# The first Walsh-Hadamard transform of a quantized feed-forward layer: one butterfly level on VectorE instead of inside the matrix products

## The chip, the cores and the metric

The kernel runs on one core of a Trainium2 chip. The metric is the device time of one execution in microseconds (us); lower is better. A profile of one execution comes beside the times. Its engines are called PE (the matrix unit, TensorE), PEld (PE's weight loads), DVE (VectorE), ACT (ScalarE), POOL (GpSimd) and SP (which here only issues transfers).

## What is computed

The input x has 128 sequences of 32 rows with 256 features, 4096 rows in all. Two layers are added to it one after the other:

```python
# layer 0: a projection with a low-rank adapter per sequence, then a mixture of
# eight experts (the best two per row) with a shared expert
x = x + L0_ffn(L0_cond(x, W, A, Bm, scalings, itok_B_0_6), gate, w1, w2, w3, ws1, ws2, ws3)

# layer 1: a mix of the 32 rows of a sequence, chosen per sequence,
# then a two-layer net on quantized values
h = einsum('bct,bcd->bdt', x, weights[itok_B_1_198])
xq = act_quant(fwht(h))                  # 256 features
h  = square(relu(xq @ weight_quant(w_up).T))
xq = act_quant(fwht(h))                  # 512 features
x  = x + xq @ weight_quant(w_down).T
```

`fwht` is the normalized fast Walsh-Hadamard transform along the features. `act_quant` divides each row by its largest absolute value, scaled to 127, and rounds. `weight_quant` rounds weights to -1, 0 and 1 times a scale.

For 256 features split into halves a and b of 128, and H the 128 by 128 Hadamard matrix, the transform is [aH + bH, aH - bH] / 16. It can also be had as [(a + b)H, (a - b)H] / 16.

## The kernel before

The kernel has three stages in one program.

- Up to about 120 us: projection, routing, and the scatter of each row to the regions of its two experts in device memory.
- Up to about 280 us: the experts' products over 72 tiles of 128 rows, in pairs, with the shared expert for all rows before and after.
- From about 280 us on: layer 1, over 16 groups of 256 rows (`G3` groups, of two tiles of 128 rows each). The change is in this stage.

In the third stage a group g goes through these functions, named here with their main tiles and lines:

- `combine` loads the two expert rows of each row (y2) and adds them to x on POOL (L634).
- `condition` forms, on PE, the mix of the sequences' rows. It comes out transposed, features on the partitions: py (called `pa` in the code, L642), two halves of 128 features, each 256 rows wide. ACT copies both halves to yT (L650).
- `quantize1` makes the transform of 256 features on PE, pf (L658): for each tile of 128 rows two products of 256 columns, one with the first half of the features and [H, H], one with the second half and [H, -H], summed in the accumulation memory. DVE then takes the row maximum m (L668, L670), the scale and its reciprocal ms (L672, L675), and ACT rounds to q1 (L679).
- `worth` squares the scales on POOL (L687, L688).
- `turn1` transposes q1 on PE (pq, L696) and ACT brings it into qT (L700).
- `up` makes the 512 hidden features, pu (L712), in two halves of bank "m". ACT takes the relu (rl, L720), DVE the square (r and pu, L721), and then the sum and the difference of the two halves, c (L722, L723), which is the outer level of the second transform.
- `outer` makes the next level on POOL: b (L730, L731).
- `quantize2` makes the remaining transform with H on PE, pr (L742), products of 128 columns. DVE forms the scale (L749, L753), ACT rounds to q2 (L756).
- `dequant` prepares the last factor on POOL (L763).
- `turn2` transposes q2 (pq, L770; ACT L772).
- `down2` makes the last product pd (L780). DVE scales it and adds x, o (L784), and the result is stored (L787).

A loop over 23 steps calls them in a software pipeline: in step s, `down2` works on group s - 7, `turn2` on s - 6, `quantize2` on s - 5, `outer` on s - 4, `up` on s - 3, `turn1` on s - 2, `quantize1` on s - 1 and `condition` on s. POOL's order is the written order (`manual_schedule`). For PE, DVE, ACT and SP the build orders the instructions by its own estimate of when they can start. On the chip each engine takes its instructions in the order built.

The accumulation memory has two buffers for each tag. Tag "t" serves py, pf and pd alike; "x" serves both pq, "m" pu, "o" pr. A tile that takes a buffer waits until the last reader of the previous one is done.

The Hadamard matrices lie in `cst`, a tile of constants: `had` is H, and `had256` gives [H, H] / 16 and [H, -H] / 16 out of three blocks of 128 columns. The constants come in two transfers (L202, L207), the second amid the loads of the rows of stage 1.

Of the kernel before, what the change touches and what calls it, by code (L numbers as in the profile page):

```python
# [7 lines left out]
F32 = mybir.dt.float32  # L8
# [4 lines left out]
ALU = mybir.AluOpType  # L13
AX = mybir.AxisListType

P = 128
D = 256
# [12 lines left out]
NSLOT = 72  # L30
# [5 lines left out]
SHARED1 = 6  # L36


C_ID, C_H, C_HS, C_TRI, C_E16, C_N16 = 0, 128, 256, 640, 704, 712
C_U, C_EREG, C_EW, C_I, C_T2 = 714, 842, 850, 858, 858 + NSLOT  # L40
NCONST = C_T2 + NT


# [1 line left out]
def tile_kernel(  # L45
# [20 lines left out]
    nc = tc.nc  # L66
# [9 lines left out]
    def bank(tag, name, shape=(P, 512), dtype=F32):  # L76
        return psum.tile(list(shape), dtype, tag=tag, name=name)
# [11 lines left out]
    cst = cpool.tile([P, NCONST], F32, name="cst")  # L89
    ident = cst[:, C_ID : C_ID + P]  # L90
    had = cst[:, C_H : C_H + P]
    had256 = [cst[:, C_HS : C_HS + D], cst[:, C_HS + P : C_HS + P + D]]
    tri = cst[:, C_TRI : C_TRI + 64].rearrange("p (e j) -> p e j", j=E)


# [16 lines left out]
    with tc.tile_pool(name="moe", bufs=1) as moe, tc.tile_pool(name="work1", bufs=2) as work1:  # L112
# [61 lines left out]
        with tc.tile_pool(name="stage", bufs=1) as stage:  # L174
# [50 lines left out]
            for k in range(3):  # L225
                for c in range(2):
# [6 lines left out]
                        start=(c == 0),  # L233
                        stop=(c == 1),
# [386 lines left out]
    work = ctx.enter_context(tc.tile_pool(name="work3", bufs=2, reuse_waits="tile"))  # L621
    TG = 2 * P
    yv = yt.rearrange("(g n p r) d -> g p n r d", n=2, p=P, r=2)

    def x_of(n):
        return xg[n // GT][:, n % GT]
# [9 lines left out]
    def condition(g):  # L636

        pa = bank("t", f"py{g}", (P, 2, TG))
        for i in range(2):
            n = 2 * g + i  # L640
            for k in range(2):
                nc.tensor.matmul(  # L642
                    pa[:, k, i * P : (i + 1) * P],
                    x_of(n)[:, k * P : (k + 1) * P],
                    bd[:, n],
                    start=True,
                    stop=True,
                )
        yT = work.tile([P, 2, TG], F32, tag="yT", name=f"yT{g}")
        nc.scalar.copy(yT, pa)  # L650
        return yT

    def quantize1(g, yT):

        pf = bank("t", f"pf{g}", (P, 2, D))
        for i in range(2):
            for k in range(2):
                nc.tensor.matmul(  # L658
                    pf[:, i],
                    yT[:, k, i * P : (i + 1) * P],  # L660
                    had256[k],
                    start=(k == 0),
                    stop=(k == 1),
                )

        ms = small.tile([P, 2, 2], F32, tag="ms", name=f"ms{g}")
        m = small.tile([P, 2], F32, tag="m", name=f"m{g}")
        nc.vector.tensor_reduce(m, pf, AX.X, ALU.max, apply_absolute_value=True)  # L668

        nc.vector.scalar_tensor_tensor(m, pf[:, :, 0], EPS, m, ALU.max, ALU.max)  # L670
        for i in range(2):
            nc.vector.tensor_scalar(  # L672
                ms[:, 0, i : i + 1], pf[:, i, 0:1], m[:, i : i + 1], 1.0 / QB, ALU.max, ALU.mult
            )
        nc.vector.reciprocal(ms[:, 1], ms[:, 0])  # L675

        q1 = work.tile([P, 2, D], F16, tag="q1", name=f"q1_{g}")
        for i in range(2):
            nc.scalar.activation(  # L679
                q1[:, i], pf[:, i], AF.Identity, bias=half, scale=ms[:, 1, i : i + 1]  # L680
            )
        return q1, ms
# [107 lines left out]
    with tc.manual_schedule(engines={mybir.EngineType.Pool}):  # L790
        for g in range(2):
            combine(g)
        y, q1, qT1, c4, b4, q2, qT2 = {}, {}, {}, {}, {}, {}, {}
        mss, s2s, m2s, dqs = {}, {}, {}, {}
        for s in range(G3 + 7):
            if 0 <= s - 2 < G3:
                s2s[s - 2] = worth(s - 2, mss.pop(s - 2))
            if 0 <= s - 6 < G3:
                dqs[s - 6] = dequant(s - 6, m2s.pop(s - 6), s2s.pop(s - 6))
            if 0 <= s - 7 < G3:  # L800
                down2(s - 7, qT2.pop(s - 7), dqs.pop(s - 7))
            if 0 <= s - 6 < G3:
                qT2[s - 6] = turn2(s - 6, q2.pop(s - 6))
            if 0 <= s - 5 < G3:
                q2[s - 5], m2s[s - 5] = quantize2(s - 5, b4.pop(s - 5), s2s[s - 5])
            if 0 <= s - 4 < G3:
                b4[s - 4] = outer(s - 4, c4.pop(s - 4))
            if s + 2 < G3:
                combine(s + 2)
            if 0 <= s - 3 < G3:  # L810
                c4[s - 3] = up(s - 3, qT1.pop(s - 3))
            if 0 <= s - 2 < G3:
                qT1[s - 2] = turn1(s - 2, q1.pop(s - 2))
            if 0 <= s - 1 < G3:
                q1[s - 1], mss[s - 1] = quantize1(s - 1, y.pop(s - 1))
            if s < G3:
                y[s] = condition(s)


def _constants():  # L820

    import numpy as np

    h = np.ones((1, 1), np.float32)
    while h.shape[0] < P:
        h = np.block([[h, h], [h, -h]])
    c = np.zeros((P, NCONST), np.float32)
    p = np.arange(P)
    e = np.arange(E)
    c[:, C_ID : C_ID + P] = np.eye(P)  # L830
    c[:, C_H : C_H + P] = h

    c[:, C_HS : C_HS + 3 * P] = np.concatenate([h, h, -h], axis=1) / 16.0
    c[:, C_TRI : C_TRI + E * E] = (e[None, :] < e[:, None]).reshape(1, -1)
    c[:, C_E16 : C_E16 + E] = p[:, None] // 16 == e[None, :]
    c[:, C_N16] = p // 16
    c[:, C_U : C_U + P] = p[:, None] < p[None, :]
    c[:, C_EREG : C_EREG + E] = e[None, :] * REG
    c[:, C_EW : C_EW + E] = e[None, :] * WCOL
    c[:, C_I : C_I + NSLOT] = np.arange(NSLOT)[None, :]  # L840

    c[:, C_T2 : C_T2 + NT] = 2 * (np.arange(NT)[None, :] * P + p[:, None]) - NY
    return c


def _layouts(inputs):
# [29 lines left out]
        "cond": v["L1_cond_weights"],  # L876
        "updown": np.stack([up, down], axis=1),
        "consts": _constants(),
    }

# [19 lines left out]
```

## Time and profile before

| what | value |
|---|---|
| median of 3 runs | 405.39 us (404.98 to 406.67) |
| profiled execution | 408.42 us, of which span 406.6 us |
| PE busy | 357.1 us (88%) |
| PEld busy | 281.4 us (69%) |
| POOL busy | 248.5 us (61%) |
| DVE busy | 227.4 us (56%) |
| ACT busy | 163.6 us (40%) |
| chain that ended last | PE 66%, POOL 15%, issue 7%, DVE 5% |
| PE's part of that chain at L658 (pf) | 6% |

The span is the time from the first to the last record of the profiled execution. Busy time is the time in which an engine executed something; an engine can be busy and still not set the time, and one that is idle may only be waiting for another. The chain that ended last is followed backwards from the last instruction, at each step to what released it. In rows of groups, "L658 PE MATMUL pf<-cst,yT" means line 658, engine, operation, output, inputs; "x128" is the number of instructions. Durations of matrix products are modelled and overlap one another, so the distance from one start to the next is the better measure.

### The profile page before, as it was taken

What the parts mean: (1) busy time and instruction counts of PE and PEld (TensorE: products, weight loads), DVE (VectorE), ACT (ScalarE), POOL (GpSimd) and SP (SyncE); (2) the same over time, 40 slices, a digit from 0 to 9 for tenths busy, and PEclk for the clock granted to TensorE, in tenths of its full rate; (3) what the DMA queues carried; (4) which work ended last, traced back from release to release, by engine and by line L of the source; (5) the groups of instructions that cost most, each with busy time, mean ns of one, the idle gap of its engine ahead of it and who ended that gap; (6) DMA issues with size and microseconds to landing.
All of it is one profiled execution on the core that took longest, in us unless ns stands there. A gap on an engine that the chain in (4) does not pass through costs nothing.

```text
span 406.6 us, 6564 instructions
## 1 busy us (share of the span) xinstructions
PE 357.1 (88%) x2055; PEld 281.4 (69%) x2055; DVE 227.4 (56%) x714; ACT 163.6 (40%) x328; POOL 248.5 (61%) x274
## 2 busy tenths in 40 slices
PE   4999999999800499999999989998999999999983
PEld 3677677565500288888787868856788998999772
DVE  1177887996500355555555545434566767757672
ACT  1122222311100034444434433421678777786863
POOL 4028888888887015555556455557898778772650
PEclk9999999999955599999999999999999999999998
DMA  6996359642222735455455431217523242010112
GB/s 230 418 409 220 133 166 248 248 141 83 94 80 96 204 107 164 147 157 164 137 151 153 147 127 71 79 35 250 179 84 119 88 140 94 33 48 28 52 53 77
DMA packets 39025, 57.49 MB, mean 141 GB/s; under 512 B 9293, under 2 KB 28879, under 8 KB 38608
## 3 DMA queue, kind: packets, MB, share of 16 engines
q1 hardware_dynamic: 31744, 39.17, 30.2%
q0 software_dynamic: 6672, 17.84, 12.2%
q8 instruction: 17, 0.28, 0.3%
q14 instruction: 16, 0.13, 0.1%
q10 hardware_dynamic: 576, 0.08, 0.1%
HBM read 33.93 MB, written 24.18 MB: 143 GB/s over the span
## 4 chain that ended last, share of the span: by engine, by line
PE 66%; POOL 15%; issue 7%; DVE 5%; DMA 3%; ACT 2%; SPq 1%; DVEq 0%; POOLq 0%; ACTq 0%
PE pg L556 16%; POOL xs L345 10%; PE pr L742 7%; PE po L582 7%; PE pf L658 6%; PE ph L265 5%; POOL pause L357 4%; PE pt_s L530 3%; PE py L642 3%; PE pd L780 3%; PE pu L712 3%; PE ph L268 3%; PE pa L253 3%; PE phd L573 2%; PE pgs L142 2%
## 5 line engine op out<-in xcount | busy, mean ns | idle before, releaser
L589 POOL DMA_INDIRECT yt<-y,to x72 | 70.1, 973 | 70.0 <-DVE cm L539 21.1
L345 POOL DMA_INDIRECT xs<-hc,dest x64 | 63.5, 992 | 40.2 <-DVE s L278 22.9
L556 PE MATMUL pg<-wall,xTs 128*128 x288 | 77.9, 395 | 3.5 <-DVE xTs L84 2.1
L556 PEld LDWEIGHTS pg<-wall,xTs 128*128 128x128 f32 x288 | 50.3, 193 | 15.4 <-issue 4.6
L564 ACT ACTIVATE sil<-pg,c 128x128 f32<-128x128 f32 x72 | 26.4, 367 | 62.5 <-PE pg L556 52.5
L565 DVE SCALAR_TENSOR_TENSOR hid<-pg,c,sil 128x128 f32<-128x128 f32 x72 | 25.0, 347 | 44.4 <-ACT sil L564 30.5
L530 PE MATMUL pt_s<-cst,xin 128*128 128x128 f32 x144 | 26.1, 286 | 25.5 <-DMA xin<-xs 25.5
L634 POOL TENSOR_TENSOR x<-x,y 128x512 f32<-128x512 f32 x32 | 40.5, 1271 | 6.2 <-PE pgs L142 4.9
L530 PEld LDWEIGHTS pt_s<-cst,xin 128*128 128x128 f32 x144 | 19.1, 147 | 30.7 <-DMA xin<-xs 26.7
L582 PE MATMUL po<-wall,hidT 128*128 x144 | 37.8, 382 | 0.0
L658 PE MATMUL pf<-cst,yT 128*128 128x256 f32 x128 | 34.9, 394 | 1.6 <-ACT yT L650 1.6
L742 PE MATMUL pr<-cst,b 128*128 128x128 f32 x256 | 34.8, 280 | 1.2 <-POOL b L731 0.7
L265 PE MATMUL ph<-WT,xT 128*128 128x264 f32 x128 | 34.9, 397 | 0.0
L269 ACT COPY hc<-ph 128x264 f32<-128x264 f32 x32 | 12.1, 378 | 50.5 <-PE ph L268 35.1
L742 PEld LDWEIGHTS pr<-cst,b 128*128 128x128 f32 x256 | 31.0, 192 | 1.7 <-POOL b L731 0.9
L265 PEld LDWEIGHTS ph<-WT,xT 128*128 128x128 f32 x128 | 25.2, 197 | 8.3 <-issue 3.7
L142 PE MATMUL pgs<-hT,ws 128*128 128x512 f32 x64 | 29.1, 598 | 0.4 <-DVE hT L84 0.4
L582 PEld LDWEIGHTS po<-wall,hidT 128*128 128x128 f32 x144 | 24.4, 190 | 2.2 <-ACT hidT L86 0.3
L658 PEld LDWEIGHTS pf<-cst,yT 128*128 128x128 f32 x128 | 21.5, 191 | 4.3 <-ACT yT L650 2.3
L756 ACT ACTIVATE q<-pr,half,sc 128x512 f16<-128x512 f32 x32 | 23.1, 779 | 2.1 <-DVE sc L753 2.1
L86 ACT COPY xTs<-pt_s 128x512 f32<-128x512 f32 x17 | 9.9, 584 | 34.6 <-PE pt_s L530 32.9
L730 POOL TENSOR_TENSOR b<-c 128x512 f32<-128x512 f32 x16 | 20.3, 1267 | 4.2 <-DVE m L749 2.7
(138 smaller groups left out, 672.9 us busy)
## 6 DMA issues: line engine op xcount, KB each, us to landing
xin<-xs SPq DMA_DIRECT2D x72, 136.0 KB
y<-yt SPq DMA_DIRECT2D x16, 512.0 KB
xT<-in_xT SPq DMA_DIRECT2D x8, 512.0 KB
x<-in_x SPq DMA_DIRECT2D x8, 512.0 KB
out<-o SPq DMA_DIRECT2D x16, 256.0 KB
wall<-in_experts SPq DMA_DIRECT2D x2, 1536.0 KB
yt<-y,to POOLq DMA_INDIRECT x72
xs<-zeros SPq DMA_DIRECT2D x8, 136.0 KB
```

The source lines that it names most:

```text
L142: nc.tensor.matmul(pg, ws13[:, k, i], hT[:, k], start=(k == 0), stop=(k == 1))
L265: nc.tensor.matmul(ph, xT[g][:, k, cols], WT[:, k], start=(k == 0), stop=False)
L345: ins = nc.gpsimd.indirect_dma_start(out=xs, out_offset=bass.IndirectOffsetOnAxis(ap=dest[:, i, n : n + 1], axis=0), in_=hc[g][:, n], in_o ...
L530: nc.tensor.transpose(pt[:, i, k], xin[:, i, k * P : (k + 1) * P], ident)
L556: nc.tensor.matmul(pg[:, i].rearrange("p a f -> p (a f)"), xT[:, i, k], wall[:, bass.ds(w + k * D, D)], start=(k == 0), stop=(k == 1),)
L564: nc.scalar.activation(sil[:, i], pg[:, i, 0], AF.Silu, scale=ci)
L565: nc.vector.scalar_tensor_tensor(hid[:, i], pg[:, i, 1], ci, sil[:, i], ALU.mult, ALU.mult)
L582: nc.tensor.matmul(po[:, i], hT[:, i], wall[:, bass.ds(w + 2 * D, D)], start=True, stop=True)
L589: ins = nc.gpsimd.indirect_dma_start(out=yt, out_offset=bass.IndirectOffsetOnAxis(ap=to[:, i : i + 1], axis=0), in_=y[:, i], in_offset=Non ...
L634: nc.gpsimd.tensor_tensor(v, v, y2[:, :, r], ALU.add)
L658: nc.tensor.matmul(pf[:, i], yT[:, k, i * P : (i + 1) * P], had256[k], start=(k == 0), stop=(k == 1),)
L742: nc.tensor.matmul(pr[:, f * P : (f + 1) * P], b[:, f, i * P : (i + 1) * P], had, start=True, stop=True,)
```

## The change

`condition` no longer copies both halves of py. ACT copies only the second half, to a new tile y1. DVE then writes the sum of the first half (read from the accumulation memory) and y1 to the first half of yT, and their difference to the second half. A DVE operation of this kind reads at most one of its inputs from the accumulation memory here, as the other sums and differences of the kernel do.

`quantize1` multiplies each half of yT by the same matrix H / 16. Each product has 128 columns and writes a part of pf of its own, so nothing is summed in the accumulation memory. There are as many products as before, four for a group. The constants lose two blocks of 128 columns, and the offsets behind them move. Lines from L649 on move by four.

```diff
-C_ID, C_H, C_HS, C_TRI, C_E16, C_N16 = 0, 128, 256, 640, 704, 712
-C_U, C_EREG, C_EW, C_I, C_T2 = 714, 842, 850, 858, 858 + NSLOT
+C_ID, C_H, C_HS, C_TRI, C_E16, C_N16 = 0, 128, 256, 384, 448, 456
+C_U, C_EREG, C_EW, C_I, C_T2 = 458, 586, 594, 602, 602 + NSLOT
...
-    had256 = [cst[:, C_HS : C_HS + D], cst[:, C_HS + P : C_HS + P + D]]
+    hads = cst[:, C_HS : C_HS + P]
...
+        y1 = work.tile([P, TG], F32, tag="y1", name=f"y1_{g}")
         yT = work.tile([P, 2, TG], F32, tag="yT", name=f"yT{g}")
-        nc.scalar.copy(yT, pa)
+        nc.scalar.copy(y1, pa[:, 1])
+        nc.vector.tensor_tensor(yT[:, 0], pa[:, 0], y1, ALU.add)
+        nc.vector.tensor_tensor(yT[:, 1], pa[:, 0], y1, ALU.subtract)
         return yT
...
                 nc.tensor.matmul(
-                    pf[:, i],
+                    pf[:, i, k * P : (k + 1) * P],
                     yT[:, k, i * P : (i + 1) * P],
-                    had256[k],
-                    start=(k == 0),
-                    stop=(k == 1),
+                    hads,
+                    start=True,
+                    stop=True,
                 )
...
-    c[:, C_HS : C_HS + 3 * P] = np.concatenate([h, h, -h], axis=1) / 16.0
+    c[:, C_HS : C_HS + P] = h / 16.0
```

## The prediction

> **What bounds the kernel now.** I read the busy tenths of the page first: PE stands at 9 in nearly all slices, from 285 us on too, where the edited functions run. Then the busy time in stretches of 7 us, about one group of 256 rows.
>
> ```profile
> 323.00:330.00 7.00, 7.00 (x62) 6.30 (x61) 4.41 (x14) 5.17 (x10) 5.27 (x8) 1.00 0.33 112
> ...
> sum 77.00, PE 76.94 PEld 69.70 DVE 52.56 ACT 58.06 POOL 55.50; mean PE 7.00 PEld 6.34 DVE 4.78 ACT 5.28 POOL 5.05
> ```
>
> PE is busy 76.94 of 77 us (302 to 379) at full clock; VectorE has 2.2 us per 7 free, ScalarE 1.7. A busy PE may still hide slack, so next the chain that ended last, for one group (start, length, what):
>
> ```profile
> 319.55 0.87 PE pu L712 x8
> 320.43 0.06 PE pq L696
> 320.48 0.49 PE pf L658 x2
> 320.97 0.17 PE pq L696 x3
> 321.14 1.35 PE pf L658 x6
> 322.49 0.89 PE py L642 x8
> 323.38 0.45 PE pq L770 x8
> 323.83 0.28 PE pr L742 x2
> 324.10 0.98 PE pd L780 x8
> 325.09 1.56 PE pr L742 x14
> 326.65 0.87 PE pu L712 x8
> ```
>
> The chain stays on PE all the way round, 7.10 us from pu to pu. The pieces give true paces, since each ends where the next starts: an fp32 instruction of 128 columns takes 0.89/8 = 0.111 us (py), one of 256 columns 1.84/8 = 0.23 (pf; 0.22 where nothing comes between). Each fp32 product is two such instructions: 128 of L658 for 64 products. The group rows (busy, mean ns | idle before) give single durations, and what the 256-column VectorE and ScalarE work resembles:
>
> ```profile
> L658 PE MATMUL pf<-cst,yT 128*128 128x256 f32 x128 | 34.9, 394 | 1.6 <-ACT yT L650 1.6
> L784 DVE SCALAR_TENSOR_TENSOR o<-pd,dq,x 128x256 f32<-128x256 f32 x32 | 14.8, 473 | 5.1 <-issue 2.9 <-POOL b L730 1.1 <-PE pd L780 1.0
> L722 DVE TENSOR_TENSOR c<-pu,r 128x512 f32<-128x512 f32 x16 | 10.9, 683 | 0.1
> L650 ACT COPY yT<-py 128x512 f32<-128x512 f32 x16 | 9.4, 590 | 11.6 <-PE py L642 11.4
> ```
>
> Last the waits, 302 to 379 us:
>
> ```profile
> POOL s L687 <- DVE ms L675: 19.9, 11, 4.1
> DVE r L721 <- ACT rl L720: 17.2, 10, 2.6
> ACT q L679 <- DVE ms L675: 11.4, 8, 1.6
> ```
>
> The others wait for one another while PE never stops: POOL 1.8 us per group for ms, ScalarE about 1.0, VectorE 1.6. That slack must carry what the change adds.
>
> **What the Trainium skill says.** (1) "TensorE: Matmul & The Clock Gate", Back-to-back issue gap: when warm, N/2.4 + 2.5 ns between products of N columns, so 109 ns at 256. The trace agrees for bf16 (pu: 0.87/8 = 109 ns); an fp32 instruction takes twice that. The same section says that a stream with a weight load per product keeps only 81 ns at 128 columns; the trace has 0.45/8 = 56 ns (pq), so weight loads do not hold this stream. (2) "VectorE: DVE Perf Modes", The TRN2 errata: an fp32 tensor_tensor takes (N + 151)/0.96 ns, 691 at 512 columns (trace: 683) and 424 at 256. (3) "Perfetto Trace Analysis", Tensor Engine Instruction: ScalarE, VectorE and GpSimd are strict FIFOs. The trace fits: ms waits behind both c operations. The last point decides this case.
>
> **The change part by part.** Line numbers are those of before.
>
> *Removed from PE:* half the columns of 128 instructions. Per group pf falls from 1.84 to 8 × 0.111 = 0.89, 0.9 us with the interleaving. If all were paid out: 16 × 0.9 = 14.4 us.
>
> *ScalarE:* the copy has 256 columns for 512. Nearest row: L269, 264 columns from PSUM, 378 ns. So 0.37 for 0.59, 0.22 less per group.
>
> *Added to VectorE:* 32 operations of 256 columns. The trace has no such tensor_tensor; bounds are L565 (128 columns, 347 ns) and L784 (256 columns, 473 ns). L722 less 256 columns at 0.96 GHz is 683 - 267 = 416 ns, near the page's 424. I take 0.42; the next one starts 0.08 earlier (the c pair starts every 0.60), so 0.34 of queue each. VectorE rises from 52.56/11 = 4.8 to 5.5 us per group.
>
> *The wait:* yT needed py and one copy, 0.1 + 0.59. Now y1, a hand-over of about 0.05, then sum and difference: 0.1 + 0.37 + 0.05 + 0.76 = 1.3 at best, plus what stands ahead in VectorE's queue. Waiting for it: pf, and by the bank "t" also pd, since py, pf and pd share two buffers. Before, pd runs inside pr, 0.05 us after the yT copy is done; the build now places it after pu or its first product. Queued behind the pair: ms (L675), for which ScalarE's q1 and POOL's worth and outer wait, and the maxima L749.
>
> *Hidden or nothing:* the constants' DMA carries 256 columns (128 KB) less; at the 418 GB/s of the page's third slice that is 0.3 us, beside PE work, so 0, at most 0.3 gained. There the build also exchanges one xa with a reciprocal and a comparison, and two L265/L268 products: 0, bounds -0.5 to 0.5. SP issues the same DMAs. POOL's queue keeps its order; its 4 × 1.27 + 3 × 0.20 = 5.7 us per group still fit.
>
> *A full group.* The build alternates two orders. I walk both by the durations above, zero being the end of pf on PE.
>
> Order A: PE has py 0.89, pq 0.45, pr 1.84, pu 0.87: 4.05, then pd. VectorE's queue up to the difference: start 0.05, m 0.60, r and pu 1.22, L670 0.07, the c pair 1.19, L672 twice 0.25, sum 0.34, L675 0.07, difference to its end 0.42: 4.21. So pd starts 0.2 late, at 4.25, and ends at 5.2. ScalarE takes rl from 3.66 (half of pu done), the pair 1.09, and only then q1, 1.02: 5.77. The pq transposes wait for it until 5.8; then 0.11, pf 0.89: 6.85. Without stalls it would be 4.05 + 0.93 + 0.22 + 0.89 = 6.1.
>
> Order B: the sum stands right behind m, the difference ends some 2.5 us after pf, long before pd; q1 comes ahead of the rl pair. No stall: 6.1.
>
> Mean 6.47 against 7.09 (308.27 to 379.22, ten groups): 0.62 × 10 = 6.2 us.
>
> *The first groups (279 to 308 us).* pf of group 0 gains 0.9 and loses 0.6 in the wait; up to the first pr at 295.9 the chain runs over VectorE, where the pair replaces an r that stood ahead of ms: together 0.7 gained. The two pf between 296 and 308 give about 0.55 each: 1.1. Sum 1.8, bounds -0.5 and 3.5.
>
> *The tail (379 to 407 us)* has no pf: 0, bounds -0.5 to 0.5.
>
> Sum: 6.2 + 1.8 = 8.0. The profiled execution takes 408.42 us (span 406.6 and 1.8 around it): 400.4. That execution lies 3.0 above the median of 405.39, so against the median 397.4.
>
> **The rivals.**
> R1, PE stays full: the stall of order A is absent since queues slide against each other. For it: VectorE is only 85% full, and r often waits today. 11 to 14.4 gained, 391 to 394.4.
> R2, VectorE's queue sets the pace in both orders: 6.8 or more per group. For it: at 5.5 of 6.5 us a strict queue has little room. Gain 0.3 × 10 or less, plus 0 to 1: 401.5 to 405.4.
> R3, slower: the loop py, y1, pair, pd, o, py through the two "t" buffers. Bare it takes 0.89 + 0.37 + 0.76 + 0.93 + 0.86 and five hand-overs of 0.05: 4.1. With the c pair (1.19), r and pu (1.22), L672 (0.25) and m (0.60) in front of the pair it is 7.4 each round, 0.3 over today: 3 us, and 0.6 in each of the first two groups: 409.6. It decides once the pair ends over 0.9 us later than walked, in every group. Against it: the build puts the pair ahead of r in every second group.
> R4, the change doesn't shorten PE: the load of fp32 weights (191 ns mean) would hold 128-column products. py and pr already go at 0.111 to 0.115 with such loads, so it is hardly possible: 8 × (0.23 - 0.19) × 16 = 5 us less at best, 400 to 405.
>
> **How the numbers follow.** A measurement tells about 0.5%, 2 us, from no change. Forecast, gain of 4 to 11 (394.4 to 401.4): 0.56. R1: 0.14. R2: 0.13, of which 0.07 lies within 2 us. R3: 0.15, with 0.01 in the band. R4: 0.02, in the faster part. Faster 0.56 + 0.14 + 0.06 + 0.02 = 0.78, same 0.08, slower 0.14. The range leaves out the best end of R1 (0.04) and R3's slower part: 392 to 406.
>
> **What would show it.** Right: pf in the chain at 0.9 us per group in place of 1.84; two alternating periods near 6.1 and 6.85; the sum and difference at 0.42 us; PE for the first time with small waits at pq (for ScalarE's q1) and pd (for the difference); POOL's wait for ms shrinking from 1.8 to about 1 us. Wrong: pf over 0.15 us an instruction (R4); periods all equal to 6.2 (R1); PE waiting for yT or for pd's buffer in every group and VectorE over 90% busy (R2, R3).

## The result, and the profile after

The changed kernel takes 400.38 us (median of 4 runs, 399.61 to 400.93), the kernel before 405.62 us in the same comparison (4 runs, 404.98 to 406.67). The ratio is 0.9867, with a 95% interval of 0.9839 to 0.9895: 5.4 us less, and 4.3 to 6.5 by the interval. The forecast was "faster", at 397.4 us in a range of 392 to 406.

The profiled execution of the changed kernel took 400.68 us (span 398.9). First the groups of instructions from 278 us on (busy us, mean ns of one | idle before, and what ended it):

```profile
L662 PE MATMUL pf<-cst,yT 128*128 128x128 f32 x128 | 18.9, 285 | 3.4 <-DVE yT L654 2.0 <-DVE yT L653 0.9 <-DVE ms L679 0.5
...
L653 DVE TENSOR_TENSOR yT<-py,y 128x256 f32<-128x256 f32 x16 | 6.7, 421 | 3.8 <-ACT y L652 3.6
L654 DVE TENSOR_TENSOR yT<-py,y 128x256 f32<-128x256 f32 x16 | 6.6, 411 | 0.0
L652 ACT COPY y<-py 128x256 f32<-128x256 f32 x15 | 5.7, 377 | 8.5 <-PE py L642 8.1
```

The products of pf have 18.9 us of busy time where they had 34.9, the sum and the difference cost 0.42 and 0.41 us, the copy 0.38. The Trainium skill's price for an fp32 tensor_tensor ("VectorE: DVE Perf Modes", The TRN2 errata: 424 ns at 256 columns by its formula) holds here to 3%.

Next the busy time in the 70 us of ten groups (PE, PEld, DVE, ACT, POOL, then the granted clock):

```profile
302.00:372.00 70.00, 67.75 (x644) 62.66 (x643) 57.73 (x170) 55.22 (x96) 52.49 (x69) 1.00 0.26 84
```

PE, which was busy 76.94 of 77 us before, now has 2.25 us of gaps in 70. VectorE is at 82%. The chain that ended last shows where the time is lost. These pieces run from the end of one pf to the end of the next ("issue" is time in which the engine waited for nothing that the profile shows):

```profile
329.38 0.89 PE py L642 x8
...
332.56 0.45 PE pu L716 x4
...
333.59 0.59 ACT rl L724
334.18 0.92 ACT q L683 x2
335.10 0.04 issue
335.14 0.34 PE pq L700 x3
335.49 0.95 PE pf L662 x8
```

Where before the chain stayed on PE all the way round, it now leaves PE after the first half of pu, passes ScalarE's relu pair and q1, and comes back for the transposes. This group takes 7.05 us (329.38 to 336.43). The next one, to 342.58, stays on PE and takes 6.15 us. So it alternates to the end of the steady part. The slow group has only 0.53 us of PE's gaps and still takes 0.90 us longer: the records of matrix products overlap one another, so a loss is read from the periods and not from the gaps. The waits from 278 to 379 us (us in total, times, longest):

```profile
POOL s L691 <- DVE ms L679: 17.6, 11, 4.0
...
PEld L700 <- ACT q L683: 3.7, 13, 0.4
...
PEld L784 <- DVE yT L654: 2.2, 4, 0.6
```

Three landmarks in both traces, the end of pf of group 5, the end of pf of group 15 and the start of the last output addition (L784 before, L788 after), split the third stage (us):

| part of the third stage | before | after | gain | forecast |
|---|---|---|---|---|
| first py to the end of pf 5 | 29.15 | 26.81 | 2.3 | 1.8 |
| ten groups, pf 5 to pf 15 | 70.95 | 65.84 | 5.1 | 6.2 |
| end of pf 15 to the last addition | 23.2 | 25.7 | -2.5 | 0 |
| sum | 123.3 | 118.4 | 4.9 | 8.0 |

The stage's 4.9 us fit the 5.2 us between the medians. The profiled execution of before had another 2.8 us in the first two stages (its first py starts at 279.12 us, that of the changed kernel at 276.33). The edit changes no operation there. With one trace of each kernel on this chip it stays open whether these 2.8 us belong to the one execution.

The tail's loss comes apart in three pieces. The landmarks are the start of the products of group 13's pr that have waited for POOL's second b ("pr 13" below), the start of the last q2, and the last output addition. In the chain of before, where pf 15 ends at 379.22 us, they are

```profile
385.98 0.49 PE pr L742 x2
...
398.17 1.27 ACT q L756 x2
...
402.39 0.48 DVE o L784
```

From the end of pf 15 to pr 13 the changed kernel takes 7.23 us in place of 6.76 (0.47). From there to the last q2 it takes 14.25 us in place of 12.19. The rest is equal. Of the 2.06 us in the second piece, 1.37 are one slow stretch of PE, in the chain of the changed kernel:

```profile
376.23 0.49 PE pr L746 x2
...
386.43 0.80 PE pr L746 x2
387.23 0.43 PE pq L774 x4
387.66 2.26 PE pr L746 x12
...
390.48 1.27 ACT q L760 x2
```

The granted clock from 386 to 391 us was 0.67. In a second profiled execution of the same kernel (experiment 5) the same three pieces of PE are

```profile
391.76 0.49 PE pr L746 x2
392.25 0.22 PE pq L774 x4
392.47 1.41 PE pr L746 x12
```

at a clock of 1.00. So 1.37 us of the tail belong to that execution, and 0.47 + 0.69 = 1.16 us came back in the second one: they belong to the kernel.

### The profile page after: what moved, and what is told of

It is laid out like the page before. It is cut to its first block, busy times and chain, and to the rows that moved or that the text cites. A ratio compares the mean times of both kernels' runs of the same rounds, so it can differ in the third digit from the quotient of the medians.

```text
span 398.9 us, 6591 instructions
## 1 busy us (share of the span) xinstructions
PE 345.7 (87%) x2055; PEld 274.4 (69%) x2055; DVE 240.5 (60%) x746; ACT 161.0 (40%) x328; POOL 249.2 (62%) x274
## 4 chain that ended last, share of the span: by engine, by line
PE 70%; POOL 12%; DVE 5%; issue 5%; ACT 4%; DMA 3%; SPq 1%; DVEq 0%; ACTq 0%; POOLq 0%
PE pg L556 17%; PE po L582 8%; PE ph L265 7%; PE pr L746 7%; POOL xs L345 7%; PE pt_s L530 4%; PE ph L268 4%; PE pa L253 4%; PE pgs L142 4%; PE pf L662 3%; PE py L642 3%; POOL pause L357 3%; PE pu L716 2%; PE phd L573 2%; DMA xT<-in_xT 2%
## 5 line engine op out<-in xcount | busy, mean ns | idle before, releaser
L565 DVE SCALAR_TENSOR_TENSOR hid<-pg,c,sil 128x128 f32<-128x128 f32 x72 | 25.1, 348 | 43.1 <-ACT sil L564 42.9
L746 PE MATMUL pr<-cst,b 128*128 128x128 f32 x256 | 35.6, 288 | 1.0 <-POOL b L734 0.5
L746 PEld LDWEIGHTS pr<-cst,b 128*128 128x128 f32 x256 | 31.8, 198 | 1.6 <-POOL b L735 0.9
L582 PEld LDWEIGHTS po<-wall,hidT 128*128 128x128 f32 x144 | 24.5, 190 | 2.2 <-ACT hidT L86 0.3
L539 DVE TENSOR_TENSOR cm<-xin,oh 128x32 f32<-128x32 f32 x36 | 6.9, 191 | 28.8 <-DMA xin<-xs 28.8
L724 ACT ACTIVATE rl<-pu 128x512 f32<-128x512 f32 x32 | 17.9, 607 | 9.9 <-PE pu L716 9.9
```

The source lines that it names most:

```text
L565: nc.vector.scalar_tensor_tensor(hid[:, i], pg[:, i, 1], ci, sil[:, i], ALU.mult, ALU.mult)
L582: nc.tensor.matmul(po[:, i], hT[:, i], wall[:, bass.ds(w + 2 * D, D)], start=True, stop=True)
L746: nc.tensor.matmul(pr[:, f * P : (f + 1) * P], b[:, f, i * P : (i + 1) * P], had, start=True, stop=True,)
```

## Experiments

The theory after the result: the shorter products take 0.9 us per group off PE, and part of it is given back because the pair changes the order in which ScalarE's and VectorE's instructions stand, and with it what PE waits for. The rivals: the pair's work itself fills VectorE (R2 of the prediction), or the chain of releases through the two buffers of bank "t" (py, pf, pd) sets the pace (R3).

The experiments ran on other chips, on which the kernel before takes 410.5 to 412.3 us, so each is given as a ratio to before on its own chip. "Period" is a group's mean from the end of pf 5 to the end of pf 15, "tail" runs from the end of pf 15 to the start of the last output addition, both in that run's own trace. Two more tails contain a stretch at a low clock like the one above: in experiments 2 and 9 the last twelve products of pr took 2.29 and 2.36 us in place of 1.41.

| kernel | ratio (95% interval) | period, us | tail, us |
|---|---|---|---|
| before | 1 | 7.10 | 23.2 |
| changed | 0.987 (0.984 to 0.990) | 6.58 | 25.7 |
| 1 products alone | 0.980 (0.974 to 0.985) | 6.26 | 23.4 |
| 2 pair alone | 1.017 (1.012 to 1.021) | 7.35 | 25.1 |
| 3 q1 ahead of the relu pair | 0.984 (0.981 to 0.988) | 6.54 | 23.8 |
| 4 both halves copied | 0.991 (0.988 to 0.995) | 6.49 | 23.0 |
| 5 changed, again | 0.988 (0.985 to 0.992) | 6.59 | 25.1 |
| 6 last relu pair first | 0.988 (0.984 to 0.992) | 6.58 | 24.5 |
| 7 pair ahead of the second square | 1.009 (1.006 to 1.012) | 7.17 | 22.6 |
| 8 pd in bank "x" | 0.977 (0.974 to 0.979) | 6.10 | 25.4 |
| 9 pd in bank "m" | 0.980 (0.976 to 0.983) | 6.16 | 25.9 |
| 10 before, pd in bank "x" | 1.006 (1.004 to 1.008) | 6.99 | 25.5 |
| 11 scales first | 1.016 (1.013 to 1.019) | 7.52 | 26.1 |
| 12 as 8, tail reordered | 0.973 (0.969 to 0.977) | 6.10 | 23.8 |

### 1 and 2: one half of the change at a time

The products alone ("..." marks what is left out of an edit):

```diff
...
-        nc.scalar.copy(y1, pa[:, 1])
-        nc.vector.tensor_tensor(yT[:, 0], pa[:, 0], y1, ALU.add)
-        nc.vector.tensor_tensor(yT[:, 1], pa[:, 0], y1, ALU.subtract)
+        nc.scalar.copy(yT, pa)
```

> This kernel has the products of 128 columns and leaves out the butterfly: ScalarE copies both halves of py to yT as before, and no sum or difference is made, so its values are not those of the layer. It is the ceiling of the change: what 128-column products are worth on PE when nothing is added to VectorE. Theory A (PE saved 0.9 us in every group, and the waits that the pair brought gave part of it back): groups of about 6.2 us without alternation, stage 3 shorter than before by some 12 us, 392 to 395 us. Theory B (the products themselves saved less than their paces say, other work on PE got slower): groups of 6.5 or more and 398 to 401 us, as the changed kernel. Whether the tail behind the last pf is longer than before without the pair is told too: if it is, the pair is not what made it longer.

The pair alone:

```diff
...
-                    pf[:, i, k * P : (k + 1) * P],
+                    pf[:, i],
                     yT[:, k, i * P : (i + 1) * P],
-                    hads,
-                    start=True,
-                    stop=True,
+                    had256[k],
+                    start=(k == 0),
+                    stop=(k == 1),
...
```

> This kernel has the sum and difference on VectorE and the smaller copy on ScalarE, and keeps the products of 256 columns with [H, H] and [H, -H]; its values are therefore not those of the layer. It adds the pair without the saving. Theory A (queues have slack as long as PE is the bound): hidden, groups of 7.1 us, 404 to 407 us. Theory B (VectorE's queue, with the pair in it, is a bound of its own near 6.6 us or more and the wait of pd and pf for the pair costs time whatever PE does): groups of 7.4 us or more, 408 us or more.

The products alone give 0.9796, 8.4 us of 410.54, and groups of 6.26 us. In the trace the third stage is 11.1 us shorter than that of before, near theory A's 12; the times show less. The pair alone costs 6.9 us, and its steady groups take exactly 7.40 us each. There the chain of every group leaves PE as in the slow group above: pu's first half, rl 0.60, q1 0.92, pq 0.34. PE's load of the pq transposes waits for q1 18 times from 300 to 378 us. So the pair does cost time, through ScalarE's order; that VectorE is full does not follow, as its instructions are not in the chain of these groups at all.

### 3: is it the order of the relu pair and q1?

```diff
...
+            with ExitStack() as stack:
+                if g + 1 in q1last:
+                    stack.enter_context(tc.issue_after(q1last[g + 1]))
-            nc.scalar.activation(rl, pu, AF.Relu)
+                nc.scalar.activation(rl, pu, AF.Relu)
```

> The changed kernel, with one constraint on ScalarE's order: the relu pair of group g is issued behind q1 of group g + 1. That takes away the order in which q1 stood behind the relu pair in every second group. In the build VectorE now has the pair behind both c operations in every group and pd behind pu. Theory A (the long groups are long only because q1 waits behind the relu pair): all groups near 6.2 us and 396 to 398 us. Theory B (the wait of pd for the difference, behind c in VectorE's queue, takes its place at once): all groups near 6.6 us, no change against the changed kernel, 399.5 to 401.5 us.

The alternation is gone, and all steady groups take 6.58 us, so the mean hardly moves. The ratio of 0.9842 is not told apart from the changed kernel's. The chain of one group shows what is late in place of q1:

```profile
346.69 0.96 PE pf L664 x8
...
347.67 0.69 DVE m L674
348.36 0.60 DVE r L730
348.96 0.61 DVE pu L730
...
349.67 0.69 DVE c L731
350.36 0.59 DVE c L732
...
351.62 0.33 DVE yT L654
...
351.99 1.05 PE pd L789 x8
```

The difference stands behind m, the squares and c in VectorE's queue. pd takes the buffer of "t" that py held, and the last reader of py is now the difference. After pd come 0.22 of pq and the next pf. This is a loop through the buffers of "t", as in R3, but a shorter one: 6.6 us in place of R3's 7.4.

### 4: another input for the pair

```diff
-        y1 = work.tile([P, TG], F32, tag="y1", name=f"y1_{g}")
+        y1 = work.tile([P, 2, TG], F32, tag="y1", name=f"y1_{g}")
...
-        nc.scalar.copy(y1, pa[:, 1])
-        nc.vector.tensor_tensor(yT[:, 0], pa[:, 0], y1, ALU.add)
-        nc.vector.tensor_tensor(yT[:, 1], pa[:, 0], y1, ALU.subtract)
+        nc.scalar.copy(y1, pa)
+        nc.vector.tensor_tensor(yT[:, 0], y1[:, 0], y1[:, 1], ALU.add)
+        nc.vector.tensor_tensor(yT[:, 1], y1[:, 0], y1[:, 1], ALU.subtract)
```

> The changed kernel, but ScalarE copies both halves of py (512 columns, 0.59 us in place of 0.37), and VectorE takes sum and difference from that copy. The buffer of tag t is free after the copy, 0.6 us after py, so pd no longer waits for the difference; the build puts pd back into pr and gives every group the same order, with q1 ahead of the relu pair. Theory A (q1 behind the relu pair and pd behind the difference are the two waits that gave the gain back): all groups 6.2 to 6.3 us, ten groups 3 to 4 us shorter than in the changed kernel, 395.5 to 398 us. Theory B (VectorE is simply too full at 5.5 us of work in a strict queue): groups stay near 6.6 us, 400 to 401 us.

ScalarE's copy now frees py's buffer early, the steady groups take about 6.5 us, and the tail is that of before. But the stretch up to pf 5 takes 30.6 us, 3.7 more than in the changed kernel, and the ratio is 0.9912. The sum and the difference are no longer always 0.42 us long. One line's instructions (duration in ns, min/median/max):

```profile
L653 DVE TENSOR_TENSOR yT<-y x16: 415/425/1376, 282.5 to 373.0; 128x256 f32<-128x256 f32 x16
```

and in the timeline (start, length) a long one beside what POOL does then:

```profile
338.12 2.63 POOL L634 TENSOR_TENSOR x<-x,y 128x512 f32<-128x512 f32 x2
...
339.75 1.28 DVE L653 TENSOR_TENSOR yT<-y 128x256 f32<-128x256 f32 x1
```

POOL's two additions end at 340.75, VectorE's operation at 341.03. Of the 32 sums and differences, nine took longer than 0.5 us, 0.77 to 1.48, and each of the nine ends 0.28 us after one of these additions of POOL. In the changed kernel, with one input in the accumulation memory, the longest of the 32 took 0.425 us. So the gain from the earlier release is mixed with this stretching, and the run can't price the release.

### 5 and 6: the changed kernel again, and its tail

Experiment 5 is the changed kernel without an edit. Experiment 6 traces the last `up` earlier and puts the second quantization of group 13 behind the relu pair of group 15 on ScalarE:

```diff
...
+            with ExitStack() as stack:
+                if g == G3 - 3:
+                    stack.enter_context(tc.issue_after(rls[G3 - 1]))
-            nc.scalar.activation(
-                q2[:, i], prs[i], AF.Identity, bias=half, scale=sc[:, i : i + 1]
-            )
+                nc.scalar.activation(
+                    q2[:, i], prs[i], AF.Identity, bias=half, scale=sc[:, i : i + 1]
+                )
...
```

> The changed kernel itself, unedited, beside the others of this call, since another chip gave the kernel before 410.5 us where the first one gave 405.6. What holds for the change must come back here: its third stage 4 to 6 us shorter than that of before in the first trace (127.5 us from the first py to the end), groups alternating between about 6.15 and 7.05 us, and a tail of about 29.9 us behind the last pf. If the alternation or the tail differ, they were a matter of that execution and not of the order built.

> The changed kernel, with ScalarE's order altered at one place behind the last pf: the relu pair of group 15 is issued ahead of q2 of group 13, as in the kernel before. All groups up to there keep their order. Theory A (the tail is 2.5 us longer than before because ScalarE takes q2 first, the outer levels of group 15 reach POOL late[...]): the tail shrinks from 29.9 to 27.3 to 28.3 us, the PE clock stays up in the last pr, 1.5 to 2.5 us faster than the changed kernel. Theory B (the tail is longer because the pair left VectorE's work in arrears at the last pf): the tail stays over 29 us and the time unchanged within 0.7 us.

The alternation comes back in 5, and so does a tail longer than before's, 25.1 us; 0.75 us of the excess lie between the last q2 and the last addition (3.70 of issue for 2.95). In 6 the stretch from pr 13 to the last q2 takes 12.99 us, against 12.89 in 5: nothing is won. The reciprocal of group 13 now stood behind c of group 15 on VectorE, and q2 waited for that. The 0.6 us between the two tails are the 0.75 above, not the edit. The theory that this relu pair is the cause fell.

### 7: the pair earlier on VectorE

```diff
...
+            with ExitStack() as stack:
+                if h and g + 3 in pair:
+                    stack.enter_context(tc.issue_after(pair[g + 3]))
-            nc.vector.scalar_tensor_tensor(pu if h else r, pu, 0.0, rl, ALU.max, ALU.mult)
+                nc.vector.scalar_tensor_tensor(pu if h else r, pu, 0.0, rl, ALU.max, ALU.mult)
...
```

together with the order of experiment 3 and the conditioning traced ahead of `up`.

> The changed kernel with both waits taken away by order alone: the relu pair of group g behind q1 of group g + 1 on ScalarE (as in the run before), and on VectorE the second square of group g behind the pair of group g + 3, so that the pair no longer stands behind both c operations; for that, condition is traced ahead of up. The instructions are the same. The build puts pd back into pr. Theory A (the loop pf, m, r, pu, c, c, scales, pair, pd, pq, pf through VectorE's queue and the buffers of tag t sets 6.6 us, and q1 behind relu the other wait; PE is the bound without them): groups of 6.2 to 6.3 us without alternation, as with the products alone, 3 to 4 us faster than the changed kernel. Theory B (VectorE too full in any order): groups of 6.5 us or more, no gain. A tail longer than 27.4 us would take part of it back.

Slower than before. The wait at the buffers of "t" did not go; it went to another of their users (waits, 300 to 378 us):

```profile
PEld py L644 <- DVE o L798: 6.2, 8, 0.8
```

py takes the buffer after pd, and the addition that reads pd now stands behind both c operations. In experiment 3 the pair was last on VectorE, here it is o, and with py, pf and pd in two buffers PE waits for either.

### 8, 9 and 10: pd out of bank "t"

```diff
-        pd = bank("t", f"pd{g}", (P, 2, D))
+        pd = bank("x", f"pd{g}", (P, 2, D))
```

> The changed kernel with the accumulation buffer of the down-projection (pd) taken from the pool of the transposes ("x") in place of the pool that py and pf share ("t"); nothing else. Theory A: what keeps the changed groups above the sum of TensorE's work (some 6.15 us) is the chain of buffer releases through "t": py waits for the pd before it to be read out, pf for py, and so the order on the queues alternates between 6.15 and 7.05 us. With pd out of that chain all groups take 6.15 to 6.3 us, ten groups 62 to 63 us in place of 65.9, and the ratio to the kernel before is 0.979 to 0.982. Theory B: the wait only moves, as the transposes of the quantized values (pq) now wait for pd's read-out in "x", and the groups stay at 6.6 us: ratio 0.985 to 0.99.

> The changed kernel with pd in the pool of the up-projection ("m"); nothing else. Theory A (only leaving "t" matters): groups of 6.15 to 6.3 us and a ratio of 0.979 to 0.982, as with pd in "x". Theory B (each pool has its own chain): the second half of pu waits for the output addition that reads pd, which stands behind the pair on VectorE, and the group takes 6.8 to 7.2 us: ratio 0.990 to 1.0.

> The kernel before with pd in "x", the control for pd in "x" in the changed kernel: 256-column products and ScalarE's one copy. Theory A: before is held by TensorE's own work, 7.0 to 7.1 us per group, and the buffers give nothing: ratio 0.995 to 1.005. Theory B: the chain through "t" costs before as much as it costs the changed kernel, and it gains 3 us as well: ratio 0.99 to 0.993.

Experiment 8 gives 0.9766, experiment 9, with "m" in place of "x", 0.9796. In 8 the chain of every group is back on PE:

```profile
330.75 0.95 PE pf L662 x8
331.70 0.89 PE py L642 x8
332.59 0.87 PE pd L784 x8
333.47 0.45 PE pq L774 x8
333.91 1.84 PE pr L746 x16
335.75 0.87 PE pu L716 x8
```

6.10 us from pf to pf, and PE is busy all of the 56 us from 310 to 366. VectorE is busy 49.88 of those 56 us, 89%, and still PE does not wait for it. That settles R2: the pair's work by itself does not bound the stage. The edit is not as pure as its one line. As the build orders by its own estimate, it also places pd right behind py in every group and q1 ahead of the relu pair. Experiment 3 had that second order without the first, at 6.58 us, so the order on ScalarE alone is not what brings 6.10. Nor is it the pair's place on VectorE: there the difference still stands behind both c operations, as in experiment 3. But pd no longer waits for it. In the timeline pd starts 2.5 us before the difference ends:

```profile
332.43 1.04 PE L784 MATMUL pd<-dnT,qT 128*128 128x256 bf16 x8
...
334.52 0.42 DVE L654 TENSOR_TENSOR yT<-py,y 128x256 f32<-128x256 f32 x1
```

In experiment 9 the order still changes from group to group (pf comes in two parts, and between them a half of pu), and the mean is 6.16 us. Leaving "t" is what 8 and 9 have in common.

In the kernel before, the same edit makes the kernel slower: groups of 6.99 us for 7.10, but a tail of 25.5 us for 23.2, and a ratio of 1.0062, just above theory A's range. So before was held by PE's own work, and the buffers count for little there. Nor do they with the short products alone (6.26 us in experiment 1, with pd in "t"). They began to count when the pair became the last reader of py. The control also has the longer tail, without any pair.

### 11: order alone

On ScalarE the order of experiment 3; on VectorE the reciprocal of the scale ahead of the next pair, and the pair ahead of an older group's squares:

```diff
...
+        with ExitStack() as stack:
+            if g - 1 in recip:
+                stack.enter_context(tc.issue_after(recip[g - 1]))
+            nc.vector.tensor_tensor(yT[:, 0], pa[:, 0], y1, ALU.add)
...
+            with ExitStack() as stack:
+                if g + 3 in pair:
+                    stack.enter_context(tc.issue_after(pair[g + 3]))
+                nc.vector.scalar_tensor_tensor(pu if h else r, pu, 0.0, rl, ALU.max, ALU.mult)
...
```

> The changed kernel with another order of issue: on ScalarE the relu of a group stands behind q1 of the next, on VectorE the scale's reciprocal ahead of the pair of the next group and that ahead of the squares of an older group; the first quantization and the conditioning are traced ahead of the up-projection. No operation is added or removed. Theory A: order is all that is left to gain, and with the scale early the groups take 6.2 to 6.3 us: ratio 0.979 to 0.983. Theory B: the squares are now late, c and with it the sums on GpSimd come later, pd's read-out on VectorE falls behind c, and the groups take 6.6 us or more: ratio 0.985 to 1.0.

Groups of 7.6 us in the steady part: the direction of theory B, and worse than its number. The chain of each group runs through VectorE from the pair to the squares, one o and both c, and only then does PE take the next half of pu (it waits for c eight times, 3.5 us). None of the orders that were tried with the pair and with pd in "t" (experiments 3, 7 and 11) came below 6.54 us.

### 12: the tail of experiment 8

Beside the edits of 6 and 8, c of group 15 stands behind the reciprocal of group 13:

```diff
...
+        with ExitStack() as stack:
+            if g == G3 - 1:
+                stack.enter_context(tc.issue_after(scs[G3 - 3]))
-        nc.vector.tensor_tensor(c[:, 0], pu, r, ALU.add)
+            nc.vector.tensor_tensor(c[:, 0], pu, r, ALU.add)
...
```

> The changed kernel with pd in the pool of the transposes, as in the experiment before, and with the last groups' order of the kernel before: the relu pair of group 15 ahead of the second quantization of group 13 on ScalarE, and on VectorE the reciprocal of group 13 ahead of the sum and difference of group 15's squares. No work is added or removed. Theory A: the 2 us that the changed kernel lost after its last pf are this order, and with it the stretch from the end of the last pf to the start of the last output addition is 23.2 to 24.0 us in place of 25.4, with ten groups at 6.1 us each; ratio 0.971 to 0.974. Theory B: the stretch is long because the pair has left VectorE in arrears, and it stays at 25 us or more; ratio 0.976 to 0.979.

The tail is 23.8 us in place of 25.4, at the same period of 6.10. From pr 13 to the last q2 it takes 12.99 us where experiment 8 took 14.53. So in that kernel 1.5 us of the tail were order. The ratio of 0.9726 (0.9686 to 0.9766) is the best of all, 11.3 us below before; its interval overlaps that of experiment 8, so against 8 the gain is shown by the trace and not by the times.

For the changed kernel itself the comparison is with experiment 3. It has the same pair and, from q2 of group 13 on, the order of before on ScalarE and VectorE. It takes 12.19 us from pr 13 to the last q2, exactly as before does (and 12.20 in experiment 1). So the 0.69 us that the changed kernel loses there are order as well. The 0.47 us ahead of it stay in experiment 3 and are gone in 12 (6.63 us). The chains show a difference: behind the last m VectorE still has both squares to take in the changed kernel and in 3, and one of them in before. That this makes the 0.47 us was not tried by itself.

## Why the prediction was right, and where it was off

It said faster and gave the direction and the mechanism; the point was 3.0 us too low, as the gain was put at 8.0 us. By its own steps:

- **Removed from PE: 0.9 us per group.** Held: pf went from 1.84 to 0.95 in the chain, 0.119 us an instruction for 0.111. R4 is out.
- **The costs on ScalarE and VectorE.** Held: copy 0.377 us (0.37), sum and difference 0.421 and 0.411 (0.42), the second one queued at 0.33 (0.34).
- **Order A, 6.85 us.** The mechanism held: q1 behind the relu pair, pq behind q1. The walk has q1 end at 5.77 us; the trace has 5.72 (329.38 to 335.10). Mis-sized is the term behind it: 0.11 us of transposes still to do, where three of the four were (0.34), and pf at 0.95 for 0.89. So 7.05. (The walk's own terms, 5.8, 0.11 and 0.89, add up to 6.80 and not to 6.85.)
- **Order B, 6.1 us.** Held: 6.15.
- **pd 0.2 us late for the difference.** Held in the main: in the slow group of the chain above PE stood still for 0.30 us before pd, and pd began 0.05 us after the end of the difference. The loads of its weights waited four times, 0.55 us each. None of this is in the chain, as q1 comes later still. Experiment 3 shows why this matters more than it looked: it is the next thing that holds PE, at nearly the same pace, once q1 is first. R3's buffers were the right place, its loop the wrong one. The loop has pf, m, squares, c, pair and pd, but not py, y1 and o, so 6.6 us and not 7.4.
- **Ten groups, 6.2 us.** 5.1. The 0.2 us by which order A was too short, in five groups, are most of it. POOL's wait for ms shrank less than foreseen, from 1.8 to 1.3 us per group (13.2 us from 302 to 372).
- **The first groups, 1.8 us.** 2.3, inside its bounds: 0.8 up to the first pr that the chain shows (0.7), and 1.5 behind it (1.1).
- **The tail, 0, bounds -0.5 to 0.5.** This step failed: -2.5 us in the profiled execution. It rested on "has no pf", but the build's order of the last groups changed with everything else (0.69), and 0.47 us came ahead of pr 13, with the cause open. 1.37 more were the clock of that one execution.
- **The 3.0 us between the profiled execution of before and its median.** It fits: the two traces differ by 2.8 us ahead of the first py. That it was a matter of that execution is not shown.

The terms account for the miss: 1.1 in the groups and 2.5 in the tail, less 0.5 in the first groups, is 3.1 us. This holds for the two traces. How much of the 1.37 us of clock is in the medians is not known, so the close agreement with the 3.0 us is in part luck.

Of the rivals, R1's pace of 6.1 to 6.2 us is possible, as experiments 8 and 9 show, but with the pair no order that was tried reached it while three users shared two buffers. It did not come about by queues that slide against each other, as R1 had it.

## What to carry to other kernels

When work moves from the engine that is full to one that has room, list which buffers the moved operation now reads last, and who takes each buffer next; here the move of pd to another pair of accumulation buffers took the ratio from 0.988 to 0.977, nearly as much again as the change itself, while it made the kernel before 0.6% slower. Where a build orders the queues, cost the edit on the changed order of the last groups too: a stage without the edited instruction can still lose. In all three orders tried here, putting one late instruction first made another late, so look for a resource to free before trying orders.

## What was not expected of the hardware

A VectorE tensor_tensor of 256 columns with both inputs in the on-chip buffer took up to 1.48 us in place of 0.42 when it ran beside POOL's two-input additions, and all nine long ones ended 0.28 us after one of them; with one input in the accumulation memory it took 0.404 to 0.425 us throughout. The Trainium skill says that POOL's interfaces to the buffer are shared with VectorE, with contention for DVE instructions with two inputs there ("GPSIMD Engine Reference", Specifications). That entry gives no size, and experiment 4 agrees with it: no operation of the pair that began during one of POOL's additions ended before that addition. Twice the operation of VectorE began first, by 0.01 and 0.10 us. It then kept its 0.42 to 0.43 us, and POOL's addition took 1.55 and 1.45 us in place of 1.27.

The granted clock fell to 0.67 from 386 to 391 us in one execution of the changed kernel, after 1.89 us in which PE was idle, and stayed at 1.00 in another with the same order and a gap as long. It also fell in the last pr of experiment 2 (0.59 from 403 to 406 us, after a gap of 1.60 us) and of experiment 9 (0.50 from 392 to 395 us, after 0.98 us), and stayed at 1.00 in that of experiment 6 after 2.13 us. So the length of the gap alone does not decide it; what does stays open.
